# Telling a static schedule about the SBUF port that VectorE and GpSimd share

## Chip, cores, metric

One core of a Trainium2 chip. Before: 2448.72 us.

## What is computed

64 graphs of 256 nodes with 256 features: layer norm and relu, three steps of a gated graph network with shared GRU weights, a residual, again layer norm and relu, one graph attention layer, a residual. All in fp32.

```python
h = relu(layernorm(x))
for i in range(3):                                   # gated graph network
    m = h @ weight[i];  aggr = A^T @ m               # A = (adj != 0)
    gi = aggr @ w_ih.T + b_ih;  gh = h @ w_hh.T + b_hh
    r, z = sigmoid(i_r + h_r), sigmoid(i_z + h_z)
    n = tanh(i_n + r * h_n)
    h = (1 - z) * n + z * h
x = x + h
# attention: e_ij = leaky(a_l h_i + a_r h_j), masked by adj; x + softmax(e) @ (relu(layernorm(x)) @ W.T)
```

## The kernel before

The kernel works on pairs of graphs, three pairs in flight. It does not write its instructions in program order: it describes every operation (engine, an estimated occupation and latency in ns, what it reads and writes), and a list scheduler places them all on a clock of its own, then emits them in that order. Each engine runs its own list in order. On the chip, engines wait for each other only where data or buffers require it.

```python
class Plan:
    def run(self, deadline):
        ...
        while done < len(self.ops):
            best = None
            for e, (free, avail) in engines.items():
                for o in avail:
                    ...
                    t = free
                    for q in o.preds:
                        t = max(t, q.start + q.occ if q.eng == e else q.end)
                    ...                                # a free buffer of its class
                    if fits and (best is None or (t, o.prio, o.seq) < best[0]):
                        best = ((t, o.prio, o.seq), o)
            ...
            o.start, o.end = t, t + o.lat
            engines[o.eng][0] = t + o.occ
            o.fn(); order.append(o)                    # emit the instruction(s)

def dve(n, fn, **kw):  plan.op("DVE", n, n + 160, fn, **kw)
def pool(n, fn, **kw): plan.op("POOL", n, n + 200, fn, **kw)
...
# GpSimd splits the first features of a pair in two parts of type fp32r (L495, L497)
pool(530, lambda ...: nc.gpsimd.tensor_copy(nodes(hi)[:, sl, :], nodes(h)[:, sl, :]), ...)
pool(1190, lambda ...: nc.gpsimd.tensor_sub(nodes(lo)..., nodes(h)..., nodes(hi)...), ...)
...
# and makes the right factors of hT in each step (L372, L376, L378): three subtractions
# the GRU update on VectorE, for each half db of the features (L542 to L552)
dve(660,  ... scalar_tensor_tensor: u = (u + b_h) * r ...)     # L542
dve(V512, ... u = u + i_n)                                     # L545
act(630,  ... u = tanh(u + b_i))                               # L547, ScalarE
dve(V512, ... d = d - u)                                       # L549
dve(V512, ... d = d * z)                                       # L550
dve(V512, ... d = d + u)                                       # L552
# TensorE then transposes d back (L566), and uses d in the next step's products (L404)
...
order = plan.run(lambda p: 32000.0 * (max(p, 0) - 0.7 * max(0, p - (NPAIR - 2))))
```

## Time and profile before

| quantity | before |
|---|---|
| time, median of 3 | 2448.72 us |
| span of the profiled run | 2446.6 us |
| TensorE idle in it | 77 us |
| period of a pair in mid-run | 74.58 us |
| TensorE's own work for a pair (spacings times counts) | 71.85 us |

The period is the distance of two adjacency conversions (L487), one per pair. The difference of the last two rows, 2.73 us a pair, is what a better order can win in mid-run. The prediction shows the lines behind the table. In profiles PE is TensorE, PEld its loads of weights, DVE VectorE, ACT ScalarE, POOL GpSimd. Added here are four groups, by line, engine, output and inputs; after the first bar stand busy us and the mean ns of one, after the second the idle us before them.

```profile
L545 DVE TENSOR_TENSOR full<-full 128x512 f32<-128x512 f32 x192 | 166.6, 894 | 2.2
L550 DVE TENSOR_TENSOR full<-full,full 128x512 f32<-128x512 f32 x192 | 152.8, 823 | 2.2
L542 DVE SCALAR_TENSOR_TENSOR full<-full,vec,full 128x512 f32<-128x512 f32 x192 | 140.8, 748 | 10.0
L497 POOL TENSOR_TENSOR round<-full,round 128x512 fp32r<-128x512 f32 x64 | 100.0, 1562 | 5.1
```

### The profile page before, as it was taken

How to read it: one execution, taken by the hardware profiler on the slowest of the kernel's cores; microseconds unless marked ns; L12 is line 12 of the kernel's file. 1: busy time of each engine (PE TensorE's matmuls, PEld its weight loads, DVE VectorE, ACT ScalarE, POOL GpSimd, SP SyncE). 2: the span in 40 equal slices, each digit the busy share in tenths (PEclk: the TensorE clock that was granted, in tenths of full speed). 3: DMA queues.
4: the chain of work that ended last, by engine and by line, in shares of the span. 5: the costliest groups of instructions: out<-in, count | busy, mean ns of one | idle time of the engine just before them, and what ended most of it. 6: DMA issues, size and time to landing. Idle time of an engine off the chain costs nothing.

```text
span 2446.6 us, 32271 instructions
## 1 busy us (share of the span) xinstructions
PE 2369.6 (97%) x12129; PEld 2061.8 (84%) x12129; DVE 1790.4 (73%) x3736; ACT 1342.6 (55%) x2627; POOL 548.0 (22%) x582
## 2 busy tenths in 40 slices
PE   8999999999999999999999999999999999999997
PEld 6878888888888888888888888888888888888885
DVE  5567777777777777777777777777777777777677
ACT  5456555555455565555555555655555555555454
POOL 3023222212222122222122221222221222212110
PEclk9999999999999999999999999999999999999998
DMA  3000000000000000000000000000000000000000
GB/s 112 1 10 27 27 26 27 27 1 27 27 27 27 20 7 27 27 27 26 1 27 27 27 26 27 1 27 27 26 27 6 22 27 26 27 18 1 9 10 18
DMA packets 53563, 55.02 MB, mean 22 GB/s; under 512 B 1680, under 2 KB 53408, under 8 KB 53408
## 3 DMA queue, kind: packets, MB, share of 16 engines
q1 hardware_dynamic: 53376, 52.96, 6.5%
q8 instruction: 95, 1.56, 0.3%
q14 instruction: 60, 0.49, 0.1%
q10 hardware_dynamic: 32, 0.01, 0.0%
HBM read 36.18 MB, written 16.78 MB: 22 GB/s over the span
## 4 chain that ended last, share of the span: by engine, by line
PE 76%; DVE 18%; ACT 4%; issue 1%; DMA 0%; POOL 0%; ACTq 0%; DVEq 0%; POOLq 0%
PE bank L404 53%; PE bank L512 7%; PE bank L644 5%; PE bank L653 5%; PE bank L566 3%; DVE full L545 3%; DVE full L550 3%; DVE full L549 2%; DVE full L414 2%; DVE small L445 2%; DVE full L542 1%; ACT full L528 1%; PE bank L473 1%; PE bank L635 1%; DVE full L552 1%
## 5 line engine op out<-in xcount | busy, mean ns | idle before, releaser
L404 PE MATMUL bank<-full,fac_hh 128*128 128x256 f32 x4032 | 1024.2, 381 | 1.5 <-ACT full L411 1.5
L404 PE MATMUL bank<-full,fac 128*128 128x256 f32 x4032 | 1022.8, 380 | 0.1
L404 PEld LDWEIGHTS bank<-full,fac_hh 128*128 128x128 f32 x4032 | 746.8, 190 | 114.2 <-ACT full L411 22.1
L404 PEld LDWEIGHTS bank<-full,fac 128*128 128x128 f32 x4032 | 748.2, 190 | 103.0 <-DVE full L376 8.9
L414 DVE TENSOR_TENSOR full<-full,bank 128x512 f32<-128x512 f32 x576 | 378.5, 683 | 331.1 <-PE bank L404 308.1
L411 ACT COPY full<-bank 128x512 f32<-128x512 f32 x576 | 329.2, 583 | 356.6 <-PE bank L404 353.6
L453 POOL TENSOR_TENSOR small<-small,nhalf 128x2 f32<-128x2 f32 x128 | 102.5, 810 | 959.8 <-DVE small L451 959.2
L372 POOL TENSOR_TENSOR full<-full 128x512 f32<-128x512 f32 x96 | 123.3, 1285 | 775.6 <-DVE full L552 594.2
L512 PE MATMUL bank<-round,round 128*128 128x256 f32 x1536 | 247.1, 303 | 1.8 <-DVE round L576 1.7
L512 PEld LDWEIGHTS bank<-round,round 128*128 128x128 f32 x1536 | 207.6, 190 | 18.1 <-DVE round L576 9.4
L528 ACT ACTIVATE full<-full,b_rz 128x512 f32<-128x512 f32 x192 | 129.0, 720 | 133.6 <-DVE full L414 133.4
L516 ACT COPY full<-bank 128x512 f32<-128x512 f32 x192 | 111.7, 582 | 122.2 <-PE bank L512 122.2
L576 DVE TENSOR_TENSOR round<-bank,round 128x512 fp32r<-128x512 f32 x128 | 85.8, 689 | 118.1 <-ACT round L574 118.0
L545 DVE TENSOR_TENSOR full<-full 128x512 f32<-128x512 f32 x192 | 166.6, 894 | 2.2
L534 ACT ACTIVATE full<-full,b_rz 128x256 f32<-128x256 f32 x192 | 91.1, 506 | 138.2 <-DVE full L414 137.8
L566 PE MATMUL bank<-ident,full 128*128 128x128 f32 x768 | 114.2, 278 | 45.3 <-DVE full L552 45.2
L547 ACT ACTIVATE full<-full,vec 128x512 f32<-128x512 f32 x192 | 135.2, 721 | 40.1 <-DVE full L545 40.1
L550 DVE TENSOR_TENSOR full<-full,full 128x512 f32<-128x512 f32 x192 | 152.8, 823 | 2.2
L566 PEld LDWEIGHTS bank<-ident,full 128*128 128x128 f32 x768 | 91.1, 141 | 72.9 <-DVE full L552 62.7
L542 DVE SCALAR_TENSOR_TENSOR full<-full,vec,full 128x512 f32<-128x512 f32 x192 | 140.8, 748 | 10.0
L460 ACT ACTIVATE full<-x,small 128x256 f32<-128x256 f32 x256 | 136.0, 592 | 14.8 <-DVE small L455 14.6
L549 DVE TENSOR_TENSOR full<-full,full 128x512 f32<-128x512 f32 x192 | 139.6, 742 | 2.2 <-ACT full L547 2.2
(78 smaller groups left out, 2343.5 us busy)
## 6 DMA issues: line engine op xcount, KB each, us to landing
x<-in_x_dram SPq DMA_DIRECT2D x32, 512.0 KB, 4.4
adj<-in_adj_dram SPq DMA_DIRECT2D x32, 512.0 KB, 3.4
out_dram<-x SPq DMA_DIRECT2D x32, 512.0 KB, 2.9
full<-in_L_gnn_w_ih_dram SPq DMA_DIRECT2D x2, 384.0 KB, 5.8
full<-in_L_gnn_weight_dram SPq DMA_DIRECT2D x3, 256.0 KB, 7.1
full<-in_L_gnn_w_hh_dram SPq DMA_DIRECT2D x2, 384.0 KB, 7.0
full<-in_L_gnn_W_dram SPq DMA_DIRECT2D x1, 256.0 KB, 5.4
rows<-in_L_gnn_a_dram ACTq DMA_DIRECT2D x1, 2.0 KB
```

The lines of the kernel that those rows point to most:

```text
L404: nc.tensor.matmul(bank.t[:, ts(s, N)], fac[t[0]][:, f, t[1], :], quarter(srcs(t), q), start=(first and n == 0), stop=True, skip_group_che ...
L411: act(A512, lambda: nc.scalar.copy(quarters(dest[e])[:, :, g, :], both(X)), r=[(X, ONE)], w=[(dest[e], (g, 2 + g))])
L414: dve(V512, lambda: nc.vector.tensor_add(quarters(dest[e])[:, :, g, :], quarters(dest[e])[:, :, g, :], both(bank)), r=[(bank, ONE)], w=[(d ...
L460: act(495, lambda k=k, nb=nb: nc.scalar.activation(nodes(dst)[:, k, :], nodes(src)[:, k, :], AF.Relu, bias=sm.t[:, 18 + nb : 19 + nb], sca ...
L512: nc.tensor.matmul(pa.t[:, ts(db, N)], nodes(part)[:, k, ts(db, P)], Ar()[:, k, :], start=(n == 0), stop=(n == len(terms) - 1))
L528: act(630, lambda s=s, RZ=RZ: nc.scalar.activation(feats(RZ[0])[:, s, :], feats(RZ[0])[:, s, :], AF.Sigmoid, bias=b_rz[:, 2 * s : 2 * s + 1]),
L542: dve(660, lambda u=u, db=db, en=en, RZ=RZ: nc.vector.scalar_tensor_tensor(u(), u(), b_h[:, en : en + 1], feats(RZ[db])[:, 0, :], op0=ALU. ...
L545: dve(V512, lambda u=u, b=U[db]: nc.vector.tensor_add(u(), u(), feats(b)[:, 1, :]), r=[(U[db], (2, 3))], w=[(U[db], (0, 1))])
L547: act(630, lambda u=u, en=en: nc.scalar.activation(u(), u(), AF.Tanh, bias=b_i[:, en : en + 1]), r=[("vec", ONE)], w=[(U[db], (0, 1))])
L549: dve(V512, lambda u=u, d=d: nc.vector.tensor_sub(d(), d(), u()), r=[(U[db], (0, 1))], w=[(hT, q)])
L550: dve(V512, lambda d=d, b=RZ[db]: nc.vector.tensor_mul(d(), d(), feats(b)[:, 1, :]), r=[(RZ[db], (2, 3))], w=[(hT, q)])
L566: nc.tensor.transpose(pt.t[:, (nb * DB + db) * P : (nb * DB + db + 1) * P], feats(hT)[:, db, ts(g * NB + nb, P)], ident)
```

## The change

The intent: the plan's clock should be true where VectorE and GpSimd want the same port to SBUF, the on-chip memory (the prediction says what is known of it). Operations of GpSimd, and those of VectorE with two SBUF inputs, may no longer overlap in the plan; two durations and the deadline spacing are adjusted with it. Cut to its core:

```diff
-    def op(self, eng, occ, lat, fn, r=(), w=(), ahead=0):
+    def op(self, eng, occ, lat, fn, r=(), w=(), ahead=0, port=False):
...
+        port = {"DVE": 0.0, "POOL": 0.0}
...
+                    if o.port:
+                        t = max(t, port["POOL" if e == "DVE" else "DVE"])
...
+            if o.port:
+                port[o.eng] = t + o.occ + 100
...
+    def dve2(n, fn, **kw):
+        plan.op("DVE", n, n + 160, fn, port=True, **kw)
     def pool(n, fn, **kw):
-        plan.op("POOL", n, n + 200, fn, **kw)
+        plan.op("POOL", n, n + 200, fn, port=True, **kw)
...           # dve becomes dve2 at the GRU update, the right factors, L455, L487, L591, L610
-                    dve(395, ... L591      ->   dve2(425, ...
-            dve(730, ... L610              ->   dve2(660, ...
...
-        order = plan.run(lambda p: 32000.0 * (...))
+        order = plan.run(lambda p: 36000.0 * (...))
```

No operation is added or removed: 12129 for TensorE, 3736 for VectorE, 2627 for ScalarE and 582 for GpSimd.

More of the change, by code (lines that the diff above doesn't have):

```diff
@@ L32 @@
 class Op:
-    __slots__ = ("eng", "occ", "lat", "fn", "bufs", "preds", "succs", "wait", "prio", "end", "start", "pair", "seq")
+    __slots__ = ("eng", "occ", "lat", "fn", "bufs", "preds", "succs", "wait", "prio", "end", "start", "pair", "seq", "port")
 class Plan:
@@ L47, in slot_class @@
         self.slots[cls] = [[0.0, t, None] for t in tiles]
-    def op(self, eng, occ, lat, fn, r=(), w=(), ahead=0):
+    def op(self, eng, occ, lat, fn, r=(), w=(), ahead=0, port=False):
         o = Op()
         o.eng, o.occ, o.lat, o.fn, o.pair, o.seq = eng, occ, lat, fn, self.pair - ahead, len(self.ops)
-        o.succs, o.prio, o.end = [], None, None
+        o.succs, o.prio, o.end, o.port = [], None, None, port
         preds, bufs = set(), set()
@@ L454, in norm_relu @@
              r=[("nhalf", ONE)], w=[(sm, (2,))])
-        dve(70, lambda: nc.vector.scalar_tensor_tensor(sm.t[:, 18:20], mv()[:, :, 0], -1.0, sm.t[:, 16:18],
+        dve2(70, lambda: nc.vector.scalar_tensor_tensor(sm.t[:, 18:20], mv()[:, :, 0], -1.0, sm.t[:, 16:18],
                                                        op0=ALU.mult, op1=ALU.mult),
@@ L486, in pair @@
         Ar = lambda: nodes(A)
-        dve(612, lambda: nc.vector.tensor_scalar(Ar(), nodes(adjt), 0.0, None, op0=ALU.not_equal),
+        dve2(612, lambda: nc.vector.tensor_scalar(Ar(), nodes(adjt), 0.0, None, op0=ALU.not_equal),
             r=[(adjt, ALL)], w=[(A, ALL)])
@@ L518, in pair @@
                     r=[(pa, ONE)], w=[(agT, (g, G + g))])
-            Tg = right_factors(nc.vector, dve, agT)
+            Tg = right_factors(nc.vector, dve2, agT)
             RZ, U = [Buf("full") for _ in range(DB)], [Buf("full") for _ in range(DB)]
@@ L541, in pair @@
                 q = (2 * db, 2 * db + 1)
-                dve(660, lambda u=u, db=db, en=en, RZ=RZ: nc.vector.scalar_tensor_tensor(
+                dve2(660, lambda u=u, db=db, en=en, RZ=RZ: nc.vector.scalar_tensor_tensor(
                     u(), u(), b_h[:, en : en + 1], feats(RZ[db])[:, 0, :], op0=ALU.add, op1=ALU.mult),
                     r=[(RZ[db], (0, 1)), ("vec", ONE)], w=[(U[db], (0, 1))])
-                dve(V512, lambda u=u, b=U[db]: nc.vector.tensor_add(u(), u(), feats(b)[:, 1, :]),
+                dve2(V512, lambda u=u, b=U[db]: nc.vector.tensor_add(u(), u(), feats(b)[:, 1, :]),
                     r=[(U[db], (2, 3))], w=[(U[db], (0, 1))])
@@ L548, in pair @@
                     r=[("vec", ONE)], w=[(U[db], (0, 1))])
-                dve(V512, lambda u=u, d=d: nc.vector.tensor_sub(d(), d(), u()), r=[(U[db], (0, 1))], w=[(hT, q)])
-                dve(V512, lambda d=d, b=RZ[db]: nc.vector.tensor_mul(d(), d(), feats(b)[:, 1, :]),
+                dve2(V512, lambda u=u, d=d: nc.vector.tensor_sub(d(), d(), u()), r=[(U[db], (0, 1))], w=[(hT, q)])
+                dve2(V512, lambda d=d, b=RZ[db]: nc.vector.tensor_mul(d(), d(), feats(b)[:, 1, :]),
                     r=[(RZ[db], (2, 3))], w=[(hT, q)])
-                dve(V512, lambda u=u, d=d: nc.vector.tensor_add(d(), d(), u()), r=[(U[db], (0, 1))], w=[(hT, q)])
+                dve2(V512, lambda u=u, d=d: nc.vector.tensor_add(d(), d(), u()), r=[(U[db], (0, 1))], w=[(hT, q)])
             last = i == L - 1
@@ L590, in pair @@
                     c = 12 + n * NB + nb
-                    dve(395, lambda k=g * NB + nb, n=n, c=c, sm=sm: nc.vector.scalar_tensor_tensor(
+                    dve2(425, lambda k=g * NB + nb, n=n, c=c, sm=sm: nc.vector.scalar_tensor_tensor(
                         nodes(sc)[:, k, :], nodes(h)[:, k, :], 1.0, va[:, n, :], op0=ALU.mult, op1=ALU.mult,
@@ L609, in pair @@
             sl = slice(g * NB, (g + 1) * NB)
-            dve(730, lambda sl=sl: nc.vector.copy_predicated(
+            dve2(660, lambda sl=sl: nc.vector.copy_predicated(
                 nodes(pm_)[:, sl, :], nodes(A).bitcast(I32)[:, sl, :], nodes(sc)[:, sl, :]),
@@ L671, in tile_gated_gnn_then_gat @@
     with tc.manual_schedule():
-        order = plan.run(lambda p: 32000.0 * (max(p, 0) - 0.7 * max(0, p - (NPAIR - 2))))
+        order = plan.run(lambda p: 36000.0 * (max(p, 0) - 0.7 * max(0, p - (NPAIR - 2))))
     return order
```

## The prediction

> **What bounds the kernel now.** I read, in this order, the first and second parts of the page, the list of waits, the chain of one stretch in mid-run, and the timelines of VectorE and GpSimd over the same ten microseconds.
>
> ```profile
> PE 2369.6 (97%) x12129; PEld 2061.8 (84%) x12129; DVE 1790.4 (73%) x3736; ACT 1342.6 (55%) x2627; POOL 548.0 (22%) x582
> PEclk9999999999999999999999999999999999999998
> PE 76%; DVE 18%; ACT 4%; issue 1%; DMA 0%; POOL 0%; ACTq 0%; DVEq 0%; POOLq 0%
> ```
>
> TensorE is busy for 97% of the span at full clock, so it is the bound, and only its idle time can be won. Yet the chain that ended last runs through VectorE for 18%. That share is not a gain on offer: the chain walks back along whatever released TensorE, also where TensorE had other work meanwhile. What TensorE really waited for is in the list of waits:
>
> ```profile
> PE bank L566 <- DVE full L552: 45.2, 56, 1.3
> PE bank L473 <- ACT full L460: 6.8, 3, 5.8
> PE bank L635 <- ACT full L619: 7.3, 5, 4.9
> ```
>
> 45.2 us of its 2446.6 - 2369.6 = 77 us of idle time is one wait: the transpose that turns the GRU's new state back (L566) waits for the last addition of the GRU update (L552). The other two lines come from the head and the tail (the list cut to the first 330 us and to the last 177 us holds them). The wait recurs once per pair of graphs: the adjacency conversion L487, one per pair, starts at 255.90 us and, 27 pairs later, at 2269.67 us, so the period is 2013.77 / 27 = 74.58 us, nearly constant.
>
> How long would TensorE need for one pair without a wait? Busy times of single matmuls overlap, so I take spacings from unbroken pieces of the chain: L404 32 in 6.91 (0.216 each), L512 8 in 0.95, all transposes 8 in 0.87, L644 8 in 1.73, L653 16 in 3.47. Counts per pair are those of the page over 32: 252 x 0.216 = 54.43; 48 x 0.119 = 5.70; transposes 24 + 8 + 8 + 4 = 44 x 0.109 = 4.79; L644 3.46; L653 3.47. Sum 71.85 us. So each period holds 74.58 - 71.85 = 2.73 us of stall, though the profile shows only 1.6 us of it as idle, since a modelled matmul end covers the first 0.16 us of each gap, and short gaps vanish.
>
> Where it arises, in one period (VectorE's line of the chain, then GpSimd's and VectorE's timelines):
>
> ```profile
> 1007.46 2.69 DVE full L545 x2
> 1010.16 1.03 DVE full L549
> ...
> 1011.21 1.64 DVE full L550
> 1012.85 0.61 DVE full L549
> ```
>
> ```profile
> 1007.24 0.69 POOL L495 CAST round<-full 128x512 fp32r<-128x512 f32 x1 [4.25 <-ACT full L460]
> 1008.01 1.60 POOL L497 TENSOR_TENSOR round<-full,round 128x512 fp32r<-128x512 f32 x1
> 1009.56 1.07 POOL L495 CAST round<-full 128x512 fp32r<-128x512 f32 x1
> 1010.71 1.59 POOL L497 TENSOR_TENSOR round<-full,round 128x512 fp32r<-128x512 f32 x1
> ```
>
> ```profile
> 1010.08 1.09 DVE L549 TENSOR_TENSOR full<-full,full 128x512 f32<-128x512 f32 x1
> 1011.21 1.64 DVE L550 TENSOR_TENSOR full<-full,full 128x512 f32<-128x512 f32 x1
> 1012.77 0.68 DVE L549 TENSOR_TENSOR full<-full,full 128x512 f32<-128x512 f32 x1
> 1013.49 0.69 DVE L550 TENSOR_TENSOR full<-full,full 128x512 f32<-128x512 f32 x1
> ```
>
> The same instructions take 0.68 us after GpSimd is through and 1.09 and 1.64 before. Three VectorE operations end at 1010.16, 1011.17 and 1012.85, each 0.55 us after a GpSimd operation ended (9.61, 10.63, 12.30): each waited for it and then ran. Excess on the chain: L545 pair 2.69 - 1.20 = 1.49, L549 0.42, L550 1.64 - 0.61 = 1.03 less its start overlap, together about 2.9 us. TensorE over 1007.70 to 1015.44: 24 matmul passes and one transpose, 24 x 0.216 + 0.109 = 5.29 us of work in 7.74 us, so 2.45 us of the 2.73 us stall is at this one place.
>
> **What the Trainium skill says.** "SBUF — State Buffer", section "Who interferes with whom": a VectorE instruction with two SBUF inputs contends with a GpSimd instruction that reads SBUF, and the second to issue waits in full; one with a single SBUF input does not contend outside the two-port modes. The trace agrees: L414, which adds a PSUM bank to an SBUF tile, takes 1.28 us for two at 1047.55 beside GpSimd's L376 and L378, as it does alone. The same section: "Issue order, not op shape, decides who blocks." The trace agrees in the other direction too: L495 takes 0.61 us alone at 10.85 us and 1.07 at 1009.56, where it met a running L545. "VectorE: DVE Perf Modes", section "Mode 2×_2P": an fp32 tensor_scalar on SBUF reads one tensor through both ports and gives twice the rate. L487 does 1024 elements in 0.69 us, as long as L545 needs for 512, which agrees; so the change is right to mark L487.
>
> **The change part by part.** It removes and adds no instruction: the same 32271 in another order. The order of each engine is fixed beforehand by a list scheduler with estimated durations; the chip only keeps data dependences. So the change adds no wait on the chip, it only alters who stands behind whom.
> 1. The port. GpSimd's operations and VectorE's with two SBUF inputs (and L487) may not overlap in the plan, with 100 ns between. What it is worth: the old plan believed the GRU update took 2 x (660 + 4 x 605) = 6.16 us; the chain shows 1006.71 to 1015.40, 8.7 us. With the true length known, either GpSimd's split is put elsewhere or other TensorE work is put in front of L566. Up to 2.45 us per pair, and 27 periods: 66 us.
> 2. What it costs: GpSimd per pair, planned: 3 x 2.4 (right factors) + 2 x 1.72 (split) + 4 x 0.9 + 0.96 = 15.2 us. VectorE's marked work per pair: 3 x (6.16 + 1.275) + 0.61 + 8 x 0.425 + 2 x 0.66 + 4 x 0.07 = 27.9 us. Sum 43.1 of 72 us, so it can be placed; VectorE's other 29 us may lie under GpSimd. All of VectorE with all of GpSimd behind it would be about 56 + 15 = 71 us, just below TensorE's 71.85, so even clumsy placing only comes near the bound. The plan also excludes the memset L583 (0.95 us), which reads nothing: needless, small.
> 3. Corrected durations: 8 x 30 ns more for L591 (trace 0.42 plus the accumulator read 0.08), 2 x 70 ns less for L610. Too small to matter by themselves.
> 4. Deadlines 36 instead of 32 us per pair: shifts ties between three pairs in flight toward the older one. It may move head and tail, where TensorE idles about 33 us (8.5 in the first 40 us, 7.6 up to 190 us, 16.6 in the last 82), by perhaps 10 us either way.
>
> Sum: I expect the stall to fall from 2.73 to about 0.7 us per pair, not to zero: 0.28 us lies elsewhere already, GpSimd's estimates remain too short (the cast is planned 530 and takes 610 to 690 ns, the subtraction 1190 and 1270 to 1280), which leaves some 0.4 us of planned exclusion violated at each split. 27 x (2.73 - 0.7) = 55 us; head and tail 0. 2448.7 - 55 = 2394 us.
>
> **Rivals.**
> A. *The collision goes, another wait comes.* Whoever has the port keeps it in this plan: the next operation of the same engine may start at once, the other engine's 100 ns later. A GpSimd train of 2.4 to 3.4 us can thus hold up a GRU update, or a GRU update the split that the next pair's propagation (L512) needs. For it: the wait list shows TensorE hitting L566 with no slack. Against: outside this one place only 0.28 us per pair are lost, with the same scheduler and similar misestimates, and two other pairs offer work. It would leave 1.2 to 2.5 us per pair: 2407 to 2443 us, within 2%.
> B. *The bound is reached.* The new plan loses 0.2 to 0.3 us per pair and the head and tail gain a little: 2446.6 - 27 x 2.5 - 10, about 2370 us.
> C. *The port was never what held TensorE*: L566 was simply placed too early. Against: the 2.9 us excess of the chain exceeds the 2.45 us stall. It would give about no change, 2440 to 2450 us.
> D. *The new order is worse* in the GAT part or in the tail by the deadline change. For it only that the order is wholly new; against, that the knob was moved together with the model. Over 2490 us is very unlikely.
>
> **Range and chances.** Faster by over 2% needs a time below about 2400 us, that is 49 us, or a stall of at most 0.9 us per pair with head and tail unchanged. My centre of 0.7 lies only just beyond that line, so the chance is a little over a half. Rivals A and C make up the rest. Predicted 2394 us, range 2369 to 2438; faster 0.56, same 0.42, slower 0.02.
>
> **What would show it.** Right: L545 and L550 fall from means of 894 and 823 ns to about 690, VectorE's busy time by about 32 x 2.9 = 93 us, GpSimd's L495 toward 610 to 690 and L497 from 1562 toward 1280; the wait of L566 for L552 falls from 45 us to under 15; the period between two L487 falls to about 72.5 us; TensorE's spacing stays at 0.216. Wrong in part (A): the means fall as said but the period stays above 73.3 us and TensorE has a new wait, probably at L512, L566 or L404. Wrong (C): the means fall, the wait of L566 stays. If the means do not fall, the plan's clock and the chip's have drifted apart, and exclusion in the plan is not exclusion on the chip.

## More of the kernel before

The metric is the time of one execution in device microseconds; medians are of several runs.

The planned start times are not handed over.

In the changed kernel the lines are numbered nine higher: L545 becomes L554, L404 becomes L413.

## The result, and the profile after

The changed kernel took 2404.81 us (median of 4, 2399.89 to 2407.04) against 2448.12 us (median of 4) in the same rounds. The ratio is 0.982, 95% interval 0.9803 to 0.9837. Ratios here are the mean of one kernel's fast runs over the mean of the other's in the same rounds, so not quite the ratio of the medians. The class is "within 2%", at its edge: 1.8% faster.

The first part of the page and the chain's shares:

```profile
PE 2352.6 (98%) x12129; PEld 2068.3 (86%) x12129; DVE 1746.6 (73%) x3736; ACT 1352.0 (56%) x2627; POOL 520.3 (22%) x582
PE 88%; DVE 8%; ACT 3%; issue 0%; DMA 0%; POOL 0%; ACTq 0%; DVEq 0%
```

VectorE's share of the chain fell from 18% to 8%. The period is 73.027 us (20 periods from 467.22 to 1927.76 us), before 74.585. The first conversion of mid-run stands at 248.14 us (before 255.90) and the last, 27 pairs later, at 2217.61 (before 2269.67). So the head gave 7.8 us, the 27 pairs 2013.8 - 1969.5 = 44.3 us, and the tail lost 8.9 us (185.8 us in place of 176.9). Sum 43.2 us, the whole difference of the spans.

What TensorE waited for (us in all, times, longest):

```profile
PE bank L662 <- ACT full L657: 19.2, 28, 0.7
PE bank L575 <- DVE full L561: 3.8, 2, 3.2
```

The old wait, the transpose for the last addition of the GRU update, fell from 45.2 to 3.8 us and is out of mid-run. A new one stands in its place, once per pair: the attention's projection (L662) waits for ScalarE's copy (L657). Now the operations of the groups shown before, and the GRU's first one, which got longer:

```profile
L551 DVE SCALAR_TENSOR_TENSOR full<-full,vec,full 128x512 f32<-128x512 f32 x192 | 166.7, 895 | 7.2
L554 DVE TENSOR_TENSOR full<-full 128x512 f32<-128x512 f32 x192 | 141.1, 761 | 1.3
L559 DVE TENSOR_TENSOR full<-full,full 128x512 f32<-128x512 f32 x192 | 127.6, 690 | 1.3
L506 POOL TENSOR_TENSOR round<-full,round 128x512 fp32r<-128x512 f32 x64 | 82.0, 1281 | 5.1
```

GpSimd's split (L506) is undisturbed, 1281 in place of 1562 ns, and so are the GRU's last operations. But L551 went from 748 to 895 ns and L554 stays at 761: a collision is left, at another place. One period, from the timelines of VectorE, GpSimd, ScalarE and TensorE (start us, us, engine, line; in brackets the idle time before and what ended it):

```profile
1033.67 2.42 DVE L551 SCALAR_TENSOR_TENSOR full<-full,vec,full 128x512 f32<-128x512 f32 x2
1036.02 1.81 DVE L554 TENSOR_TENSOR full<-full 128x512 f32<-128x512 f32 x2
```

```profile
1034.16 1.38 POOL L381 TENSOR_TENSOR full<-full 128x512 f32<-128x512 f32 x1 [14.68 <-ACT full L486]
1035.62 1.06 POOL L385 TENSOR_TENSOR full<-full,full 128x256 f32<-128x256 f32 x1
```

```profile
1033.51 0.57 ACT L486 COPY full<-bank 128x512 f32<-128x512 f32 x1
...
1037.27 1.38 ACT L556 ACTIVATE full<-full,vec 128x512 f32<-128x512 f32 x2 [2.21 <-DVE full L554]
1038.56 1.05 ACT L657 COPY full<-bank 128x512 f32<-128x512 f32 x2
```

```profile
1039.17 1.99 PE L662 MATMUL bank<-wT,full 128*128 128x256 f32 x8 [0.69 <-ACT full L657]
```

Read from below: TensorE waits for the copy L657; in ScalarE's list the copy stands behind two tanh (L556), which idle 2.21 us for L554; L554 is late because L551 took 2.42 us for two (1.41 for two at 1005.14 us, where GpSimd was idle) beside GpSimd's right factors. GpSimd began them at 1034.16 us, 0.08 us after the copy L486 had made their input (1033.51 + 0.57). It had been idle for 14.68 us.

And where had the plan put them? From the scheduler itself, its own clock in us from the pair's conversion:

```text
plan's clock       start    end
ACT  L486 copy     55.85   56.50    input of GpSimd's factors ready
DVE  L551 (2nd)    55.66   56.48
DVE  L554 ... L561 56.32   61.92    GRU update, port held almost throughout
DVE  L385          61.76   62.26    the last on the port
POOL L381          62.20   63.59    right factors
```

The plan knows the port and puts the factors off by 5.7 us (62.20 - 56.50). The emitted program has no wait that says so, and on the chip they start 0.08 us after their input.

### The profile page after: what moved, and what is told of

Same layout as the page of the kernel before. It is cut to its first block, busy times and chain, and to the rows that moved or that the text cites. A ratio compares the mean times of both kernels' runs of the same rounds, so it can differ in the third digit from the quotient of the medians.

```text
span 2403.4 us, 32216 instructions
## 1 busy us (share of the span) xinstructions
PE 2352.6 (98%) x12129; PEld 2068.3 (86%) x12129; DVE 1746.6 (73%) x3736; ACT 1352.0 (56%) x2627; POOL 520.3 (22%) x582
## 4 chain that ended last, share of the span: by engine, by line
PE 88%; DVE 8%; ACT 3%; issue 0%; DMA 0%; POOL 0%; ACTq 0%; DVEq 0%
PE bank L413 69%; PE bank L521 8%; PE bank L662 5%; PE bank L575 3%; DVE full L551 3%; ACT full L556 2%; DVE full L554 1%; DVE full L648 1%; PE bank L482 1%; PE bank L644 1%; ACT full L657 1%; PE bank L611 1%; PE bank L653 1%; PE bank L345 0%; DVE full L423 0%
## 5 line engine op out<-in xcount | busy, mean ns | idle before, releaser
L413 PE MATMUL bank<-full,fac_hh 128*128 128x256 f32 x4032 | 1002.3, 379 | 0.6 <-ACT full L486 0.2
L413 PE MATMUL bank<-full,fac 128*128 128x256 f32 x4032 | 992.0, 379 | 0.0
L413 PEld LDWEIGHTS bank<-full,fac 128*128 128x128 f32 x4032 | 753.8, 190 | 96.6 <-DVE full L385 0.7
L413 PEld LDWEIGHTS bank<-full,fac_hh 128*128 128x128 f32 x4032 | 747.2, 190 | 93.6 <-DVE full L423 0.6
L381 POOL TENSOR_TENSOR full<-full 128x512 f32<-128x512 f32 x96 | 129.7, 1351 | 1204.5 <-DVE full L561 772.4
L462 POOL TENSOR_TENSOR small<-small,nhalf 128x2 f32<-128x2 f32 x128 | 91.8, 726 | 554.3 <-DVE small L460 552.6
L556 ACT ACTIVATE full<-full,vec 128x512 f32<-128x512 f32 x192 | 135.0, 723 | 100.5 <-DVE full L554 98.6
L551 DVE SCALAR_TENSOR_TENSOR full<-full,vec,full 128x512 f32<-128x512 f32 x192 | 166.7, 895 | 7.2
L554 DVE TENSOR_TENSOR full<-full 128x512 f32<-128x512 f32 x192 | 141.1, 761 | 1.3
L662 PE MATMUL bank<-wT,full 128*128 128x256 f32 x512 | 118.6, 385 | 19.2 <-ACT full L657 19.2
L662 PEld LDWEIGHTS bank<-wT,full 128*128 128x128 f32 x512 | 95.0, 190 | 42.2 <-ACT full L657 30.4
L561 DVE TENSOR_TENSOR full<-full,full 128x512 f32<-128x512 f32 x192 | 127.7, 692 | 2.1
L559 DVE TENSOR_TENSOR full<-full,full 128x512 f32<-128x512 f32 x192 | 127.6, 690 | 1.3
L558 DVE TENSOR_TENSOR full<-full,full 128x512 f32<-128x512 f32 x192 | 127.3, 689 | 0.4 <-ACT full L556 0.4
L583 ACT CAST round<-bank 128x512 fp32r<-128x512 f32 x128 | 69.6, 594 | 101.0 <-PE bank L575 101.0
```

The costliest lines, as they stand in the source:

```text
L381: eng.tensor_sub(T.t[:, : 2 * N].rearrange("p (c n) -> p c n", c=2), q[:, :, 1, :], b.t[:, : 2 * N].rearrange("p (c n) -> p c n", c=2))
L413: nc.tensor.matmul(bank.t[:, ts(s, N)], fac[t[0]][:, f, t[1], :], quarter(srcs(t), q), start=(first and n == 0), stop=True, skip_group_che ...
L551: dve2(660, lambda u=u, db=db, en=en, RZ=RZ: nc.vector.scalar_tensor_tensor(u(), u(), b_h[:, en : en + 1], feats(RZ[db])[:, 0, :], op0=ALU ...
L554: dve2(V512, lambda u=u, b=U[db]: nc.vector.tensor_add(u(), u(), feats(b)[:, 1, :]), r=[(U[db], (2, 3))], w=[(U[db], (0, 1))])
L556: act(630, lambda u=u, en=en: nc.scalar.activation(u(), u(), AF.Tanh, bias=b_i[:, en : en + 1]), r=[("vec", ONE)], w=[(U[db], (0, 1))])
L561: dve2(V512, lambda u=u, d=d: nc.vector.tensor_add(d(), d(), u()), r=[(U[db], (0, 1))], w=[(hT, q)])
```

## The experiments

For the numbers expected I wrote a replay: it takes a plan's order and runs each engine's list with the durations of the two traces, the data dependences, and an exclusive port. It is an estimate. It gave 2464 and 2404 us for the two kernels (measured 2448 and 2405); the traces of both went into it, so these two are no independent test. Both plans believe in the same period, 71.616 us, and in 2355 and 2354 us in all: for the plan's own clock the change is worth 1 us.

**Theories.** 1: collisions on the port at one place make the stall, and the port rule wins by keeping the plan's clock true. 2: the deadline spacing wins, the port rule is beside the point. 3: each new order meets more or fewer harmful collisions by luck, and the rule only improves the odds. After the first eight runs came 4: the plan's exclusion isn't kept on the chip, because an idle GpSimd starts when its data are there.

All runs have three rounds against the kernel before, and four executions. Results are correct unless said.

| run | time, us | ratio to before | period, us |
|---|---|---|---|
| the changed kernel | 2404.81 | 0.9820 | 73.03 |
| e1 port rule alone | 2414.53 | 0.9859 | 73.37 |
| e2 deadline 36 alone | 2451.49 | 1.0008 | 74.73 |
| e3 split only writes (wrong result) | 2391.01 | 0.9761 | 72.54 |
| e4 factors only write (wrong result) | 2370.92 | 0.9680 | 72.07 |
| e5 changed, deadline 30 | 2371.99 | 0.9681 | 71.95 |
| e6 before, deadline 30 | 2378.25 | 0.9709 | 71.90 |
| e7 before, latency 240 in the plan | 2384.95 | 0.9736 | 72.26 |
| e8 changed, no 100 ns gap | 2403.74 | 0.9822 | 73.17 |
| e9 changed, deadline 30, latency 200 | 2366.69 | 0.9662 | 71.82 |
| e10 changed, with a real wait | 2372.17 | 0.9692 | 72.08 |
| e11 port rule alone, with a real wait | 2378.38 | 0.9716 | 72.08 |
| e13 changed, GpSimd's true durations | 2421.44 | 0.9893 | 73.92 |

Periods are means over 20 to 22 pairs between 400 and 2000 us.

### e1 and e2: the parts of the change alone

```diff
 e1, from the changed kernel
-    order = plan.run(lambda p: 36000.0 * ...
+    order = plan.run(lambda p: 32000.0 * ...
-    dve2(425, ... / dve2(660, lambda sl ...
+    dve2(395, ... / dve2(730, lambda sl ...
 e2, from the kernel before
-    order = plan.run(lambda p: 32000.0 * ...
+    order = plan.run(lambda p: 36000.0 * ...
```

> The changed kernel with the deadline spacing back at 32 us and the two old durations: the port rule alone. Theory 1 (the port rule itself wins, by keeping the plan's clock true): about 2413 us, from a replay of the plan's order with the durations of the two traces and an exclusive port; certainly under 2425. Theory 2 (the deadline spacing wins, the port rule is beside the point): 2445 us or more, like before.

> The kernel before with the deadline spacing at 36 us and nothing else. Theory 1: no gain; the same replay gives a loss, about 2508 us, and the port collisions stay (mean of the GRU update's first addition above 800 ns). Theory 2: about 2405 us like the changed kernel.

The port rule alone gave 2414.5 us, 1.4% below before; the deadline alone gave nothing (1.0008, interval 0.9992 to 1.0025). Theory 2 falls. In e2 collisions stayed, as expected (mean of the GRU's first addition 841 ns), if not all at the old place: VectorE's own right factors are caught too (L376 800 ns, before 425). The replay was right for e1 (2413) and wrong for e2 (2508 against 2451); why it missed there I did not pursue. The scheduler alone, run without the chip, already plans 72.77 us a pair for e2, against 71.616. But e1 doesn't show what theory 1 says. Two of its groups, GpSimd's cast and the GRU's first addition:

```profile
L504 POOL CAST round<-full 128x512 fp32r<-128x512 f32 x64 | 61.0, 952 | 106.6 <-ACT full L469 106.6
L554 DVE TENSOR_TENSOR full<-full 128x512 f32<-128x512 f32 x192 | 168.2, 904 | 2.1
```

904 and 952 ns, before 894 and 838: the split still runs into the GRU update, with the port rule in the plan. So the 35 us of e1 came without that collision going away; the order around it is another, and it costs TensorE less.

### e3 and e4: the collisions taken out, the order kept

```diff
 e3, from the kernel before (order of the plan unchanged)
+    def fill_hi(sl=sl, h=h):
+        nc.gpsimd.tensor_copy(scratch[:, 0:2], nodes(h)[:, sl, 0])   # reads two elements
+        nc.gpsimd.memset(scratch, 0.5)
+    def fill_lo():
+        nc.gpsimd.memset(scratch, 0.25)
+        nc.gpsimd.memset(scratch, 0.5)
-    pool(530, lambda ...: nc.gpsimd.tensor_copy(hi, h), ...)
-    pool(1190, lambda ...: nc.gpsimd.tensor_sub(lo, h, hi), ...)
+    pool(530, fill_hi, ...);  pool(1190, fill_lo, ...)
-    terms = [... for part in (hi, lo) ...]
+    terms = [... for part in ((A, A) if i == 0 else (hi, lo)) ...]
 e4, from the changed kernel: GpSimd's right factors likewise
+    eng.tensor_copy(T.t[:, 0:4], <one element of each quarter of b>)
+    eng.memset(T.t[:, : 2 * N], 0.25);  eng.memset(T.t[:, : 2 * N], 0.5)
+    ...                                  # and two memsets for each of T2, T4
```

> The kernel before in its old order, but GpSimd's split of a pair's first features reads two elements of SBUF and otherwise only writes, into a scratch tile, for about as long; the first propagation takes the adjacency tile in place of the split (wrong result on purpose). Theory 1 (the collision of this split with the GRU update is the whole stall of 2.45 us): the period between two adjacency conversions falls from 74.58 to about 72.3 us, the time to about 2380 us, and the update's means fall to about 690 ns. Rival (the transpose is merely placed too early, or any GpSimd operation blocks VectorE): the period stays above 74 us.

> The changed kernel in its own order, but GpSimd's right factors read four elements and otherwise only write, for about as long (wrong result on purpose). Theory 1b (what is left of the stall, 73.03 - 71.85 = 1.18 us a pair, comes from the one collision left, of the right factors with the GRU update's first two operations): period about 71.9 us, time about 2366 us. Rival (the stall left has another cause, such as ScalarE's queue by itself): period stays at 72.8 to 73.0 us and the time at 2395 to 2405.

Both results are wrong on purpose, as they had to be. In e3 the period fell from 74.58 to 72.54 us and the time to 2391 us (expected 72.3 and 2380). The old wait of TensorE, 45.2 us before, is all but gone (L572 and L558 are the old L566 and L552):

```profile
PE bank L572 <- DVE full L558: 1.5, 2, 1.3
```

GpSimd was at work at the same place, and VectorE passed it by (GpSimd's and VectorE's timelines of e3; L556 and L555 are the old L550 and L549):

```profile
988.37 0.53 POOL L498 MEMSET scratch<- 128x512 f32 x1
988.95 0.53 POOL L501 MEMSET scratch<- 128x512 f32 x1
```

```profile
988.30 0.69 DVE L556 TENSOR_TENSOR full<-full,full 128x512 f32<-128x512 f32 x1
988.91 0.68 DVE L555 TENSOR_TENSOR full<-full,full 128x512 f32<-128x512 f32 x1
```

So theory 1 is right about the old stall: 74.58 - 72.54 = 2.04 us of its 2.73 came from GpSimd reading SBUF here. In e4 the period fell from 73.03 to 72.07 us: 0.96 of the changed kernel's 1.18 us come from the one collision left. GpSimd's work was about as long as the work it replaced (0.27 + 3 x 0.53 = 1.86 us in e3 for 0.61 + 1.27), so it is the reading and not the time that went. In e3 the first propagation also no longer depends on the split; that can't be the effect, since in the kernel before no propagation starts until 10 us after the split has ended (1022.12 and 1012.30 us), and the one that reads this split, by the plan's order, only at 1043.61 us; the list of waits has none for the split.

### e5, e6, e7, e9: other numbers in the plan

```diff
 e5, from the changed kernel          -  36000.0 *     +  30000.0 *
 e6, from the kernel before           -  32000.0 *     +  30000.0 *
 e7, from the kernel before, in dve() -  n + 160       +  n + 240
 e9, from the changed kernel          -  36000.0 *     +  30000.0 *
                 in dve() and dve2()  -  n + 160       +  n + 200
```

> The changed kernel with one number altered, the deadline spacing 30 us instead of 36. The replay (the plan's order, the traces' durations, an exclusive port) gives 2370 us, against 2404 for the changed kernel and 2464 for the one before (measured 2405 and 2448). If the replay, and with it theory 1, holds: 2360 to 2385. If deadlines of 36 were needed for the gain (theory 2): 2405 or more.

> The kernel before, without the port rule, with the deadline spacing 30 us. Replay 2392 us. Theory 1 in its strong form (without the port rule the plan can't avoid collisions): above 2430. Theory 3 (each new order meets more or fewer collisions by luck, and the port rule only improves the odds): 2375 to 2415.

> The kernel before, without the port rule, deadlines of 32 us, with one number altered: the plan counts 240 ns instead of 160 ns from the end of a VectorE operation to its use by another engine. Replay 2377 us. Theory 1 in its strong form: above 2430. Theory 3: below 2400, as good as the port rule or better.

> The changed kernel with deadlines of 30 us and a VectorE latency of 200 ns in the plan, the best few-number variant found by the replay: 2366 us, a period of 71.84 us (TensorE's own work is 71.85). If the replay holds: 2355 to 2380 and no stall left in mid-run. If the chip has waits that the replay does not know: above 2390.

One number in the kernel before, without any knowledge of the port, won 2.9% (e6) or 2.6% (e7), more than the whole change. Theory 1 in its strong form falls, and theory 3 fits. The collisions of these two orders lie elsewhere: in e6 the GRU's additions are free without the port rule (L545 684 ns, L549 684), and the attention's scores are caught instead (L591 568 ns, before 420), where TensorE does not wait for long (2.2 us in all). With the same deadline spacing the port rule helped each time, but unevenly: 2451 to 2405 us at 36 (e2 to the changed kernel), 2449 to 2415 at 32 (before to e1), 2378 to 2372 at 30 (e6 to e5); at 36 and 30 the two durations changed with it. e9 is the fastest kernel, 3.4% below before, with a correct result. I found it by replaying some 600 settings of the changed kernel's plan, so it is a search result, not a proof of the rule. TensorE's busy time in the same 1500 us of mid-run, first in the kernel before, then changed, then e9 (the columns are the stretch, its length, and busy us with the instructions of TensorE, weight loads, VectorE, ScalarE and GpSimd, then clock and DMA):

```profile
400.00:1900.00 1500.00, 1467.64 (x7560) 1281.38 (x7559) 1125.35 (x2342) 830.50 (x1624) 343.61 (x362) 1.00 0.07 22
```

```profile
400.00:1900.00 1500.00, 1485.85 (x7725) 1313.11 (x7724) 1110.53 (x2388) 855.12 (x1656) 326.98 (x365) 1.00 0.07 22
```

```profile
400.00:1900.00 1500.00, 1500.00 (x7860) 1340.47 (x7859) 1102.70 (x2424) 880.94 (x1697) 334.26 (x376) 1.00 0.07 23
```

In e9 the profile shows no idle time of TensorE in this stretch, and its period of 71.82 us agrees with the 71.85 worked out for TensorE's own work. By this measure only the head, the tail, or less work for TensorE are left to win.

### e10 and e11: a wait that the chip keeps

Where the plan put a GpSimd operation later only because VectorE held the port, GpSimd first copies one word of what that VectorE operation wrote (36 times in e10, 61 in e11, 187 ns each). The data dependence makes GpSimd wait.

```diff
+    if o.port:
+        o.after = lastdve if e == "POOL" and port["DVE"] > t else None
...
+    if o.after is not None:
+        self.hold(*o.after.out)      # nc.gpsimd.tensor_copy(held, <one word of its output>)
     o.fn()
```

> The changed kernel, same plan, but where the plan put a GpSimd operation later only because VectorE held the port, GpSimd first reads one word of what that VectorE operation wrote, so that the chip must wait too. Theory 4 (the plan's exclusion is not kept on the chip: GpSimd, idle, starts as soon as its data are there, ahead of its planned time and into the GRU update): the collision left goes, the means of the update fall to 690-750 ns, 2368 us by the replay, 2360 to 2385 allowed. Rival (GpSimd's durations in the plan are too short, as the prediction said): no gain, 2395 or more.

> The port rule alone (deadlines of 32 us, old durations; measured 2414.5 us, with the split of the features still in collision with the GRU update), with the same real wait. Theory 4: 2370 us by the replay, 2360 to 2390 allowed, and GpSimd's split back at 620 and 1280 ns. Rival: still above 2400.

e10 came to 2372.2 us where the changed kernel has 2404.8, with the same plan; its period is 72.08. GpSimd's timeline at the place of the collision, with VectorE's last operation before it (L396, L400 are the right factors, L566 the GRU's first operation in this kernel):

```profile
1024.86 0.19 POOL L207 COPY held<-full 128x1 f32<-128x1 f32 x1 [21.41 <-DVE full L400]
1025.00 1.28 POOL L396 TENSOR_TENSOR full<-full 128x512 f32<-128x512 f32 x1
```

```profile
1024.38 0.41 DVE L400 TENSOR_TENSOR full<-full,full 128x256 f32<-128x256 f32 x1
```

```profile
L566 DVE SCALAR_TENSOR_TENSOR full<-full,vec,full 128x512 f32<-128x512 f32 x192 | 138.2, 746 | 7.2
```

The factors now start after VectorE's L400, where the plan wanted them, and L566 is back from 895 to 746 ns. The period is that of e4 (72.07), which took the collision out, but here the result is correct. That is theory 4.

e11 also gained, 2414.5 to 2378.4 us, but my side condition failed: GpSimd's split did not get its 620 and 1280 ns (they are 1031 and 1589). It now waits until the first half of the update is through, then collides with the second:

```profile
1053.27 1.66 POOL L521 TENSOR_TENSOR round<-full,round 128x512 fp32r<-128x512 f32 x1
```

```profile
1053.72 2.78 DVE L574 TENSOR_TENSOR full<-full,full 128x512 f32<-128x512 f32 x2
1056.42 2.36 DVE L576 TENSOR_TENSOR full<-full,full 128x512 f32<-128x512 f32 x2
```

VectorE loses nearly as much in e11 as before: the means of these two, 900 and 838 ns, exceed 684 by 370 ns together, x192 = 71 us; in the kernel before, L545, L549 and L550 (894, 742, 823) exceed it by 407 ns, x192 = 78 us. Yet its period is 72.08 us, 0.23 above TensorE's own work, and before 2.73. In this kernel a collision costs only where TensorE has nothing else to do. It also means that e11's gain is not shown to come from the exclusion being kept; only e10 shows that.

### e8 and e13: the reason that the prediction gave

```diff
 e8,  from the changed kernel   -  port[o.eng] = t + o.occ + 100     +  port[o.eng] = t + o.occ
 e13, from the changed kernel   -  pool(530 / 1190 / 900, factors 1195, 605, 605
                                +  pool(615 / 1270 / 670, factors 1275, 735, 735
```

> The changed kernel without the 100 ns that the plan leaves after an operation on the port. Replay 2431 us, that is, a worse order, though its own clock moves by 0.2 us in 2354. If the replay holds: 2415 to 2445. If the gap is of no consequence: 2400 to 2410.

> The changed kernel with GpSimd's durations in the plan set to those of the trace (615, 1270, 1275, 735, 735, 670 ns in place of 530, 1190, 1195, 605, 605, 900) and no other edit. The prediction's reason for the stall left (these estimates are too short, so that planned exclusion is violated by some 0.4 us): a gain, 2370 to 2395 us. Theory 4: no gain of that kind, only one more order; the replay says 2422 us.

With GpSimd's true durations in the plan the kernel got slower, 2421.4 us. The GRU's operations have means of 682 to 687 ns there (747 for the first), so no collision with the update is left. Others are: VectorE's right factors (L381, L385, L387) have 791, 714 and 677 ns there, in the changed kernel 684, 420 and 445. TensorE waits instead for ScalarE, in two new places, by the list of waits:

```profile
PE bank L644 <- ACT full L556: 23.6, 27, 0.9
PE bank L653 <- ACT full L525: 13.6, 27, 0.5
```

What makes ScalarE late in that order I did not follow up. Its time does not test the prediction's reason cleanly: the scheduler, run without the chip, plans 73.65 us a pair and 2409 us in all for it, where it planned 71.616 and 2354 for the changed kernel. With longer durations under exclusion this order is slower on the plan's own clock, and the chip's 73.92 us lie close to it. e8 missed the replay (2431) and came out like the changed kernel (2403.7 us). Its order is another, and the collision left catches other operations (L554 841 ns, L558 767), so the equal times may be chance.

## Why the prediction was right, and where it was not

The measured 2404.8 us lies in the range of 2369 to 2438; the centre, 2394, was 11 us low, and "faster by over 2%" was given the larger chance (0.56) but did not come about.

- **Bound, and ceiling of the gain: right.** TensorE's own 71.85 us per pair was reached in e9 (71.82).
- **The stall at one place, 2.45 of 2.73 us: right in kind.** e3, which takes only that collision away, recovers 2.04 us. Rival C (the transpose merely stood too early) falls with e3.
- **The expected signs: half.** L550 went to 690 and the split to 1281 as said, the wait for L552 to 3.8 us. L545 stayed at 761 instead of 690; VectorE's busy time fell by 44 us instead of 93, since the collision moved to L551. The period, 73.03, lies between the sign for right (about 72.5) and that for rival A (above 73.3).
- **The term that was mis-sized: the stall left.** It was put at 0.7 us per pair and is 73.03 - 71.85 = 1.18 between 400 and 2000 us. Over the 27 periods that the prediction summed it is 1969.5 / 27 - 71.85 = 1.09; 27 x 0.39 = 10.5 us of the miss of 11. Head and tail (7.8 us won, 8.9 lost) nearly cancelled; the prediction put them at zero, with 10 us either way, and did not argue that they cancel. Rival A, a collision with a new wait behind it, took a part of it, though not at L512, L566 or L404 as guessed.
- **The reason for it: wrong.** The prediction said that GpSimd's estimates are some 80 ns too short, so that exclusion is violated by 0.4 us at each split. The split is undisturbed (L506 at 1281 ns); the collision left is that of the right factors, which start when their input is there, 5.7 us ahead of their place in the plan. What violates the exclusion is that the port exists only in the plan. The prediction had the premise ("the chip only keeps data dependences"), but named the conclusion only in its last sentence, for the case that the means do not fall, and left it out of the sum. e10 adds the missing wait and wins 33 us more. e13, with the durations corrected, still has operations running together that its plan keeps apart (L385 at 714 ns), so short estimates are not all of it. That it is 17 us slower decides nothing here, since its plan is slower on its own clock.
- **Part 4, deadlines: right that they hardly act by themselves** (e2), wrong that their range is small. At 30 us instead of 32 (e6) they are worth 71 us in the kernel before. A deadline acts only through the order that it gives; whether a smaller spacing gives better orders as a rule is open.

Not settled: why e13 and e2 have the waits that they have (their plans are longer, which may be a part of it), and whether e6 is luck. Both kernels were fastest at 30 us and slower at 32 and 36, which luck need not explain; three pairs of orders at three spacings do not make a distribution.

## What to carry to other kernels

A static order fixes who stands behind whom on one engine and nothing else; a delay for a shared resource that no semaphore enforces is not kept by an engine that has nothing else to do, so add a real dependence (e10) or do not count on the delay. When the bound engine has other work at a place, such a collision is nearly free (e11), so look at what the bound engine waits for, not at how long the blocked engine is busy. Before crediting a model in a scheduler, change an unrelated number of it a few times: here one such number (e6) moved the time more than the model did.

## What the Trainium skill lacked or had wrong

- "SBUF — State Buffer", "Who interferes with whom", holds, also in the point that a GpSimd operation that only writes does not block a VectorE operation with two SBUF inputs: 0.68 and 0.69 us beside memsets in e3, and 1.64 us beside a reading one in the kernel before. It does not say how a blocked operation looks in a profile: the wait is inside the busy time, not in the idle time. GpSimd's cast reads 0.61 us free and 1.07 caught, VectorE's L545 0.67 us free and up to 1.76 caught, and the list of waits has no entry for it.
- "Perfetto Trace Analysis", "GPSIMD Engine Instruction", advises to treat GpSimd's spans as unreliable and to use the spacing of starts. Here both nearly agree: the subtraction reads 1.27 us free, and its start is 1.25 us before the next (1053.34 to 1054.59 in the changed kernel); the cast reads 0.61 us, with 0.69 to the subtraction that needs its result.
- No page says that an order planned with exclusive use of the port is not kept on the chip without a dependence: GpSimd started 0.08 us after its input, 5.7 us ahead of plan, and 33 us of the kernel's time depended on it (e10).
